# Taps of small levels for keys and values in common, wide additions of exps, and an unscaled token variance

## The chip, the cores and the metric

The kernel runs on one core of a Trainium2 chip. The metric is the device time of one execution in microseconds. Before the change the median of three runs was 3230.94 us (3228.27 to 3233.72). TensorE (PE) does matrix products, with weight loads (PEld) beside them; VectorE (DVE), ScalarE (ACT) and GpSimd (POOL) work on tiles; SyncE (SP) and GpSimd issue most of the DMA.

## The reference, cut to what matters

Eight images of 256 channels and 32 x 32 pixels go through two layers. Layer 0 is attention over a pyramid of keys and values, and it is where the change lies:

```python
q = einsum('bchw,oc->bohw', x, q_w)             # 8 heads of 32 channels
kv = einsum('bchw,oc->bohw', x, kv_w)           # key map, value map
def pooled(t):
    outs = []
    for i, r in enumerate([1, 2, 3, 6]):        # sides 32, 16, 11, 5
        p = average_pool(t, round(32 / r))
        p = p + depthwise_3x3(p, dconv_w[i], dconv_b[i])
        outs.append(p.reshape(B, C, -1))
    return concatenate(outs, axis=2)            # 1024 + 256 + 121 + 25 = 1426
k = layernorm(pooled(k_map).transpose(0, 2, 1), norm_w, norm_b)
v = layernorm(pooled(v_map).transpose(0, 2, 1), norm_w, norm_b)
att = softmax(q_g @ k.T * 32 ** -0.5) @ v       # per head, then a head mix, proj, residual
```

Here x is normalised by groups first. Layer 1 is single-head attention over the 1024 tokens of each image (width 256), then a network of eight experts that all run for every token, weighted by a gate. Everything is float32.

## The kernel before

The 256 channels lie on 128 partitions in two halves, c = 0 and 1. All queries, keys and values of layer 0 are made by batch b (one image). One batch is 45 steps: two halves c, two halves of the 1024 queries, and eleven key chunks of 128 (a unit is one c and one query half), plus one tail step for the last keys of all four units. In a step `scores` (line 1596) makes four heads' products into the single score buffer `sc` in PSUM, ScalarE takes their exp into a `pt` tile of 128 x 4 x 512 (six buffers), and `values` (1606) of the step before is accumulated in `pv`. So the next score has to wait for the exp to have read `sc`. Keys stand in tiles `kn`, value tokens in `vt`.

Beside the steps runs background work: preparing the next batch, and layer 1 of the last one (`layer1` at 1778, `outputs` at 1832). These are generators, called threads. The class `Flow` (662) is a planner: it keeps an estimated clock per engine and per tile, resumes the thread whose next operation is estimated to be ready, and so writes one fixed order for every engine. `step` (916) runs threads between scores within a credit of TensorE time; `finish` (929) runs them until something that is needed exists. Where it foresees a wait of over 1.8 us on TensorE, `warm` (844) writes filler, products of constants. Each engine then runs its order strictly one after another. Every recorded operation has line 675, so the profile tells them apart by tile names.

For a batch, `prepare` (1463) normalises x and pools it to sides 11 and 5; `maps` (1184) forms four maps by matmul (m = 2, 3 are values, 0, 1 keys) over pixels and the two small pooled levels; ScalarE copies each from PSUM into a map tile and writes the middle tap with bias into `acc`; `halve` (1163) makes the side-16 level on GpSimd. `convolve` (1357) calls `taps` (1327): eight operations of VectorE per level and map, each acc += tap * shifted map, for four levels, so each depends on the one before. The first batch has its own order (`first_maps`, `first_keys`, `first_taps`); TensorE does the large convolution of its keys.

`by_tokens` (1384) turns four key chunks of `acc` to tokens by transposes, takes their statistics on VectorE (`statistics`, 1369) and scales them on ScalarE. The reciprocal root is a power on GpSimd; `rstd` (1024) multiplies the summed variance by 1/C and adds eps on VectorE before it. `value_tokens` and `key_tokens` (1547, 1560) do so in three groups, of which g = 2 has the small levels.

For the softmax sums, an accumulating DMA from GpSimd's queue adds each odd chunk's exps to those of the even chunk before (`add`, 1651; `tail_add`, 1643), and `sums` (1658) adds the six resulting tiles on VectorE, each in two operations of 128 x 1024, before one product by ones. The first four units sum on TensorE instead.

After the last step the rest of layer 1 and the experts run. A branch at the end would repeat everything in a general form if the sums were out of bounds.

Of the kernel before, what the change touches and what calls it, by code (L numbers as in the profile page):

```python
# [25 lines left out]
NT = NK - (NKC - 1) * P  # L26
NE = 8
SCALE0 = DH ** -0.5
SCALE1 = C ** -0.5
FILLER = 5  # L30
# [15 lines left out]
KEY_CHUNKS = [(i * P, min(P, NK - i * P)) for i in range(NKC)]  # L46
# [102 lines left out]
def layer0_general(tc, kit, nb, x, t1, consts, consts8, vecs, q_t, kv_t, proj_t, gqk_t):  # L149
    nc = tc.nc  # L150
    T = kit.tile
    with ExitStack() as ctx:
# [189 lines left out]
        def transpose_values(b):  # L342
            acc = vs.pop(b)
            for i in range(0, NKC, 2):
                ps = T(psum, [P, 512], "sm")
                part = KEY_CHUNKS[i : i + 2]
# [14 lines left out]
        def global_token(b):  # L361
# [22 lines left out]
            for kc, (k0, w) in enumerate(KEY_CHUNKS):  # L384
                nc.tensor.transpose(ps[:w, kc * 8 : kc * 8 + 8], pg[:, k0 : k0 + w], ident[:HEADS, :HEADS])
            pt = T(work, [P, NKC * 8], "gpt")
            last, lw = (NKC - 1) * 8, KEY_CHUNKS[-1][1]
# [5 lines left out]
            for kc, (k0, w) in enumerate(KEY_CHUNKS):  # L393
                nc.tensor.matmul(
                    ps[:HEADS, :C],
                    lhsT=pt[:w, kc * 8 : kc * 8 + 8],
                    rhs=vext[:w, kc, :, 0::2, :],
                    start=kc == 0,
                    stop=kc == NKC - 1,
                )  # L400
# [144 lines left out]
        def attend(n, background, steps):  # L545
# [4 lines left out]
            for half in range(2):  # L550
# [14 lines left out]
                for kc, (k0, w) in enumerate(KEY_CHUNKS):  # L565
# [381 lines left out]
def attention(tc, kit, f, outer, ended, nb, consts, x, t1, t2, hn, bounds, vecs, q_t, kv_t, proj_t, gqk_t, wqk, wqkv, vecs1, w1_d, w1c, gate_d, wrc, vecs2, bnvec, w2_d, h2d, between, pre, held):  # L947
# [6 lines left out]
    with ExitStack() as ctx:  # L954
# [73 lines left out]
        def mix():  # L1028
# [79 lines left out]
            for c in range(2):  # L1108
                f.ve.tensor_scalar(mt[:, c, :], raw[:, c, :], vec[:, V_NW + c : V_NW + c + 1], None, ALU.mult)
# [20 lines left out]
        made = [0]  # L1130
# [32 lines left out]
        def halve(p, small_p, c, acc):  # L1163
# [7 lines left out]
            l2 = small_p.rearrange("p (h w) -> p h w", h=16)  # L1171
            f.pool.tensor_tensor(l2, t2[:, 0::2, :], t2[:, 1::2, :], ALU.add)
            pooling.clear()
            yield act(small_p)
            f.act.activation(
                acc[:, HW : OFFS[2]],
                small_p,
                AF.Identity,
                bias=db(c, 1),
                scale=mid[:, c * 4 + 1 : c * 4 + 2],  # L1180
            )
            halved.append(acc)

        def maps(xp):

            for m in (2, 3, 0, 1):
# [5 lines left out]
                acc = T(work, [P, NK], "acc", bufs=3)  # L1192
                for s0, w in MAP_SLICES:
                    if s0 >= HW:
                        yield until(lambda: len(done) >= len(todo) - 1)
                        f.spawn(halve(p, p[:, HW : OFFS[2]], c, acc), 1)
# [3 lines left out]
                    for k in range(2):  # L1200
# [6 lines left out]
                        )  # L1207
                    f.act.activation(p[:, s0 : s0 + w], ps[:, :w], AF.Copy)
                    for s, n in enumerate(SIDES):
                        a, z = max(OFFS[s], s0), min(OFFS[s] + n * n, s0 + w)  # L1210
                        if a < z:
                            f.act.activation(
                                acc[:, a:z],
                                ps[:, a - s0 : z - s0],
                                AF.Identity,
                                bias=db(c, s),
                                scale=mid[:, c * 4 + s : c * 4 + s + 1],
                            )
# [8 lines left out]
        pmaps = [T(pool_, [P, NK], f"map{i}") for i, pool_ in enumerate((between, work))]  # L1227
        for t in pmaps:
            f.split(t, 512, HW)
        first, large, whole, pooled, asked, halved = {}, [], [], [], [], []  # L1230
# [13 lines left out]
        def first_maps(xp):  # L1244


            for m in range(4):
                if m < 2:
                    p = T(work, [P, 4, 512], "pt", bufs=6).rearrange("p j q -> p (j q)")
                    acc = T(l1, [P, NK], "v") if m else T(work, [P, NK], "kn", bufs=3)  # L1250
                else:
                    p = pmaps[m - 2]
                    acc = T(work, [P, NK], "acc", bufs=3)
                for t in (p, acc):
                    if t is not p or m < 2:
                        f.split(t, 512, HW)
                first[m] = p, acc
            for m, s0 in [(m, s0) for m in (2, 3) for s0 in (0, 512)] + [
# [11 lines left out]
                for k in range(2):  # L1270
# [7 lines left out]
                small_levels = s0 > HW and m < 2  # L1278
                f.act.activation(
                    ptail[:, m, s0 - HW : s0 - HW + w] if small_levels else p[:, s0 : s0 + w], ps[:, :w], AF.Copy  # L1280
                )
                for s, n in enumerate(SIDES):
                    a, z = max(OFFS[s], s0), min(OFFS[s] + n * n, s0 + w)
                    if a < z and (m >= 2 or s):
                        f.act.activation(
                            acc[:, a:z],
                            ps[:, a - s0 : z - s0],
                            AF.Identity,
                            bias=db(c, s),
                            scale=mid[:, c * 4 + s : c * 4 + s + 1],  # L1290
                        )
                if s0 == 512:
                    f.spawn(halve(p, ptail[:, m, :256] if m < 2 else p[:, HW : OFFS[2]], c, acc), 0)
                if s0 == 512:
# [5 lines left out]
            whole.append("maps")  # L1300
# [26 lines left out]
        def taps(c, s, p, acc, base=0):  # L1327
            n, o = SIDES[s], OFFS[s]
            pin = p[:, o - base : o - base + n * n].rearrange("p (h w) -> p h w", h=n)
            pout = acc[:, o : o + n * n].rearrange("p (h w) -> p h w", h=n)  # L1330
            for tap in range(9):
                if tap == 4:
                    continue
                dy, dx, y0, y1, x0, x1 = windows(tap, n)
                o_ap = pout[:, y0:y1, x0:x1]
                yield ve(pin[:, y0 + dy : y1 + dy, x0 + dx : x1 + dx], o_ap)
                f.ve.scalar_tensor_tensor(
                    o_ap, pin[:, y0 + dy : y1 + dy, x0 + dx : x1 + dx], dw(c, s, tap), o_ap, ALU.mult, ALU.add
                )

        def first_taps():
# [5 lines left out]
            yield until(lambda: whole)  # L1347
            for m in (0, 1, 2, 3):
                p, acc = first[m]
                for s in range(1, 4):  # L1350
                    if s == 1:
                        yield until(lambda: acc in halved)
                    yield from taps(m % 2, s, *((ptail[:, m, :], acc, HW) if m < 2 else (p, acc)))
                whole.append(m)
            done.extend(first[m][1] for m in (2, 3, 0, 1))

        def convolve():

            for m in range(4, 4 * nb):
                yield until(lambda: len(todo) > m)  # L1360
                c, p, acc = todo[m]
                for s in range(4):
                    if s == 1:
                        yield until(lambda: acc in halved)
                    yield from taps(c, s, p, acc)
                    read[0] += s == 0
                done.append(acc)

        def statistics(st, n, eps, mean=None):
# [7 lines left out]
            f.ve.tensor_tensor(var, st[:, :, 2], st[:, :, 5], ALU.add)  # L1377
# [3 lines left out]
            rstd(r, var, eps, 1.0 / C)  # L1381
            return r

        def by_tokens(accs, dst, k0):

            chunks = KEY_CHUNKS[k0 : k0 + 4]
            st = T(work, [P, 4, 6], "tst", bufs=3)
            f.pool.memset(st, 1.0)
            for i in range(0, 4, 2):
                span = slice(chunks[i][0], sum(chunks[i + 1]))  # L1390
# [6 lines left out]
                w = chunks[i + 1][1]  # L1397
                if w == P:
                    f.act.activation(dst[:, i : i + 2, :], ps.rearrange("p (u c) -> p u c", u=2), AF.Copy)
                else:  # L1400
                    f.act.activation(dst[:, i, :], ps[:, :C], AF.Copy)
                    f.act.activation(dst[:w, i + 1, :], ps[:w, C:], AF.Copy)
# [60 lines left out]
        def prepare(b):  # L1463
# [42 lines left out]
            else:  # L1506
                yield from maps(xp)
# [1333 lines left out]
```

## Time and profile before

| | us |
|---|---|
| median of three runs | 3230.94 |
| profiled execution, its own time | 3231.56 |
| its span, first to last instruction | 3229.8 |
| start to first exp of layer 0 | 84.7 |
| first to last exp | 1755.8 |
| last exp to end | 1389.3 |
| TensorE busy in the span | 3071.1 |
| VectorE busy in the span | 2350.0 |
| ScalarE busy in the span | 1628.2 |

The profile is of one execution. A group is named by the tiles that it writes and reads, as `acc<-map,vec,acc` for a tap, `pt<-pt,pt` for an addition of exps, `sc<-q,kn` for scores, `sm<-con` for filler. A float32 product shows as two records. "Idle before" is time in which an engine had nothing running ahead of an operation, and the name behind the arrow is what ended that. Work on an engine that is not the bound costs time only if another engine waits for it.

### The profile page before, as it was taken

To read this page: it belongs to the slowest core of one execution; us is meant where nothing else is said; L and a number is where in the kernel's file an instruction comes from. 1 tells how busy PE (TensorE), PEld (TensorE's weight loads), DVE (VectorE), ACT (ScalarE), POOL (GpSimd) and SP (SyncE) were. 2 spreads that over 40 slices of the span, in tenths; PEclk is the share of its full clock that TensorE was granted. 3 is DMA by queue.
4 is the path that set the end of the run, shared out by engine and by line. 5 is a ranking of instruction groups with operands and counts; after the bars stand their busy time and mean duration, and the time that the engine had idled before them with its cause. 6 is when DMAs were issued, how large, how long until landed. Compare 5 with 4: busy or idle time off the path is not lost.

```text
span 3229.8 us, 57102 instructions
## 1 busy us (share of the span) xinstructions
PE 3071.1 (95%) x22958; PEld 1782.2 (55%) x22958; DVE 2350.0 (73%) x4196; ACT 1628.2 (50%) x2164; POOL 1183.1 (37%) x1273
## 2 busy tenths in 40 slices
PE   7889799989999999999999999999999999999998
PEld 4323233334333333433433367776888888888887
DVE  6973888878888788898544444445887888887776
ACT  3757666556666566656655423334333333334443
POOL 3323223132242232322121120003855556567766
PEclk9999999999999999999999999999999999999999
DMA  1367765565665575666776652224444345320000
GB/s 54 82 134 185 141 144 121 134 148 110 155 133 121 133 158 105 146 137 141 168 160 134 147 210 92 79 72 154 150 150 141 142 162 169 131 81 24 20 14 21
DMA packets 123346, 396.04 MB, mean 123 GB/s; under 512 B 15280, under 2 KB 41208, under 8 KB 99840
## 3 DMA queue, kind: packets, MB, share of 16 engines
q0 software_dynamic: 28608, 179.85, 28.7%
q1 hardware_dynamic: 90960, 210.46, 19.1%
q8 instruction: 183, 3.00, 0.4%
q10 hardware_dynamic: 3504, 1.99, 0.2%
q14 instruction: 91, 0.75, 0.1%
HBM read 129.77 MB, written 97.03 MB: 70 GB/s over the span
## 4 chain that ended last, share of the span: by engine, by line
PE 51%; DVE 5%; issue 2%; ACT 1%; POOL 1%; DMA 1%; DVEq 0%; ACTq 0%; POOLq 0%
PE bank L675 21%; PE sm L675 10%; PE y L675 10%; PE sx L675 3%; PE sc L675 3%; PE pv L675 3%; DVE h L675 2%; DMA pt<-pt 1%; ACT pt L675 1%; DVE u L675 1%; DVE pt L675 1%; DVE c L675 1%; POOL t L675 0%; DVE t L675 0%; DVE acc L675 0%
## 5 line engine op out<-in xcount | busy, mean ns | idle before, releaser
L675 ACT ACTIVATE pt<-sc 128x2048 f32<-128x2048 f32 x352 | 660.8, 1877 | 284.5 <-PE sc L675 226.8
L675 DVE SCALAR_TENSOR_TENSOR acc<-map,vec,acc 128x961 f32<-128x961 f32 (+3 forms) x960 | 561.2, 593 | 33.7 <-ACT acc L675 7.6
L675 DVE TENSOR_TENSOR pt<-pt,pt 128x1024 f32<-128x1024 f32 x280 | 350.7, 1298 | 193.6 <-DMA pt<-pt 177.9
L675 PE MATMUL sc<-q,kn 32*128 32x512 f32 (+1 forms) x3072 | 419.3, 647 | 68.6 <-ACT pt L675 62.2
L675 PE MATMUL pv<-pt,vt 128*32 128x512 f32 x2816 | 382.0, 615 | 2.2 <-ACT vt L675 2.2
L675 ACT ACTIVATE h<-h,bnvec 128x512 f32<-128x512 f32 x432 | 326.7, 805 | 64.9 <-DVE h L675 57.4
L675 POOL TENSOR_TENSOR rstd<-rstd,mhalf 128x4 f32<-128x4 f32 (+2 forms) x88 | 103.5, 1177 | 690.9 <-DVE rstd L675 625.6
L675 ACT ACTIVATE p1c<-bank 128x256 f32<-128x256 f32 x216 | 82.5, 382 | 541.9 <-PE bank L675 541.3
L675 POOL DMA_DIRECT2D pt<-pt x160 | 144.9, 909 | 441.2 <-ACT pt L675 331.6
L675 DVE TENSOR_TENSOR h<-p1c,bank 128x512 f32<-128x512 f32 x216 | 147.2, 681 | 197.4 <-PE bank L675 191.9
L675 PEld LDWEIGHTS sc<-q,kn 32*128 32x128 f32 (+1 forms) x3072 | 113.6, 178 | 246.6 <-ACT pt L675 137.0
L675 DVE TENSOR_TENSOR h<-u,bank 128x256 f32<-128x256 f32 (+1 forms) x432 | 219.8, 550 | 7.4
L675 POOL TENSOR_TENSOR tm<-h,tm 128x256 f32<-128x256 f32 x190 | 217.6, 1145 | 14.9
L675 PEld LDWEIGHTS pv<-pt,vt 128*32 128x32 f32 x2816 | 56.0, 109 | 275.2 <-issue 259.5
L675 DVE TENSOR_TENSOR h<-h,gate 128x1024 f32<-128x1024 f32 x128 | 194.4, 1519 | 0.9 <-ACT h L675 0.5
L675 POOL TENSOR_TENSOR tm<-h 128x512 f32<-128x512 f32 x95 | 121.5, 1279 | 186.0 <-ACT h L675 186.0
L675 PE MATMUL y<-t,s3e 128*128 128x256 f32 x768 | 187.0, 380 | 2.0 <-POOL t L675 2.0
L675 PE MATMUL sm<-y,t 128*32 128x256 f32 (+1 forms) x1992 | 182.9, 387 | 3.7 <-DVE res L675 2.5
L675 PE MATMUL bank<-t,s1e 128*128 128x256 f32 x726 | 176.6, 379 | 0.0
L675 POOL TENSOR_TENSOR t<-h 128x512 f32<-128x512 f32 x98 | 124.5, 1270 | 132.4 <-DVE h L675 100.1
L675 DVE TENSOR_TENSOR u<-h,bank 128x512 f32<-128x512 f32 x216 | 148.5, 687 | 23.3 <-PE bank L675 0.5
L675 PE MATMUL bank<-h,w2e 128*128 128x256 f32 (+1 forms) x480 | 161.5, 466 | 2.4 <-DVE h L675 2.4
(374 smaller groups left out, 5513.8 us busy)
## 6 DMA issues: line engine op xcount, KB each, us to landing
pt<-pt POOLq DMA_DIRECT2D x160, 1024.0 KB, 7.8
h<-h SPq DMA_DIRECT2D x175, 512.0 KB
xi<-in_x_dram SPq DMA_DIRECT2D x16, 512.0 KB
t<-t SPq DMA_DIRECT2D x8, 1024.0 KB
res<-t SPq DMA_DIRECT2D x32, 256.0 KB
t<-res SPq DMA_DIRECT2D x32, 256.0 KB
hn<-res SPq DMA_DIRECT2D x32, 256.0 KB
hn<-hn SPq DMA_DIRECT2D x16, 512.0 KB
```

The lines of the kernel that those rows point to most:

```text
L675: ins = fn(*args, **kwargs)
```

## The change

It has three parts.

1. The three small levels of keys and values of one channel half lie together. A tile `small{c}` of 836 columns has, for each level of side n, the value map of n rows, one row of zeros, and the key map of n rows: 2n+1 rows (33 x 16, 23 x 11, 11 x 5). Its accumulator is `sacc{c}`. One tap then covers both maps. GpSimd sets the zero rows (`small_maps`), `join` writes the middle tap with bias once all four contributions are there, and `small_taps` runs after the four large levels of the batch. Large maps and their `acc` shrink to 1024 columns. The last two key chunks become 121 and 25 keys instead of 128 and 18, so that they are the levels of side 11 and 5. Value tokens g = 2 wait until the units of the batch before have passed chunk 3; `vt` has five buffers in place of six, `tst` two in place of three.
2. `sums` adds a pair of exps over all 2048 columns in one operation (121 rows for the last).
3. For tokens, the summed variance is not divided by C; eps * C is added in an operation that was there, and the power is taken of it at once. Normalised tokens are then smaller by sqrt(C) = 16: the exps' scale for keys and the weights `mt` behind the values hold the factor `SPREAD`.

```diff
-NT = NK - (NKC - 1) * P
+NT = 25
+NS = (0, 528, 781, 836)
+SPREAD = C ** 0.5
-KEY_CHUNKS = [(i * P, min(P, NK - i * P)) for i in range(NKC)]
+ALL_CHUNKS = [(i * P, min(P, NK - i * P)) for i in range(NKC)]
+KEY_CHUNKS = [*ALL_CHUNKS[:-2], (OFFS[2], OFFS[3] - OFFS[2]), (OFFS[3], NT)]
...
+        def small_maps(b, c):
+            yield until(lambda: len(convolved) >= 2 * b - 2 + c + 1)
+            t = smaps[b, c] = T(work, [P, NS[3]], f"small{c}")
+            for s in range(1, 4):
+                f.pool.memset(level(t, s)[:, SIDES[s] : SIDES[s] + 1, :], 0.0)
+            counts[b, c] = 0
+            f.spawn(join(b, c), 1)
+        def join(b, c):
+            yield until(lambda: counts[b, c] == 4 and (b == 0 or {(b - 1, 0), (b - 1, 1)}.issubset(marks)))
+            yield act(smaps[b, c])
+            acc = T(work, [P, NS[3]], f"sacc{c}")
+            for s in range(1, 4):
+                a, z = NS[s - 1], NS[s]
+                f.act.activation(acc[:, a:z], smaps[b, c][:, a:z], AF.Identity, ...)
+            joined[b, c] = acc
+        def copy_small(ps, b, c, keys):
+            for s in (2, 3):
+                ...
+                f.act.activation(level(smaps[b, c], s, keys), src.rearrange("p (h w) -> p h w", w=n), AF.Copy)
+            counts[b, c] += 1
...
-        def taps(c, s, p, acc, base=0):
+        def taps(c, s, p, acc):
+            rows = 2 * n + 1 if s else n
...
+        def small_taps(b):
+            for c in range(2):
+                yield until(lambda: (b, c) in joined)
+                for s in range(1, 4):
+                    yield from taps(c, s, smaps[b, c], joined[b, c])
+                convolved.append((b, c))
...
-            for m in range(4, 4 * nb):
-                yield until(lambda: len(todo) > m)
-                c, p, acc = todo[m]
-                for s in range(4):
-                    if s == 1:
-                        yield until(lambda: acc in halved)
-                    yield from taps(c, s, p, acc)
-                    read[0] += s == 0
-                done.append(acc)
+            for b in range(1, nb):
+                for m in range(4 * b, 4 * b + 4):
+                    yield until(lambda: len(todo) > m)
+                    c, p, acc = todo[m]
+                    yield from taps(c, 0, p, acc)
+                    read[0] += 1
+                    done.append(acc)
+                yield from small_taps(b)
...
-            f.ve.tensor_tensor(var, st[:, :, 2], st[:, :, 5], ALU.add)
+            if mean is None:
+                f.ve.tensor_tensor(var, st[:, :, 2], st[:, :, 5], ALU.add)
+            else:
+                f.ve.scalar_tensor_tensor(var, st[:, :, 2], eps * C, st[:, :, 5], ALU.add, ALU.add)
...
-            rstd(r, var, eps, 1.0 / C)
+            if mean is None:
+                rstd(r, var, eps, 1.0 / C)
+            else:
+                f.pool.tensor_tensor(r, var, kit.mhalf[:, 0:1].to_broadcast([P, n]), ALU.pow)
...
+            if g == 2:
+                yield until(lambda: len(convolved) >= 2 * b + 2 and (b == 0 or spent[0] >= 4 * b))
+                accs = [joined[b, c] for c in range(2)]
...
-            f.act.activation(pt[:w], t[:w], AF.Exp, scale=SCALE0)
+            f.act.activation(pt[:w], t[:w], AF.Exp, scale=SCALE0 * SPREAD)
...
-                for j in range(0, 4, 2):
-                    s = pairs[0][:, j : j + 2, :]
-                    yield ve(s, pairs[i])
-                    f.ve.tensor_tensor(s, s, pairs[i][:, j : j + 2, :], ALU.add)
+                s = pairs[0][: rows[i]]
+                yield ve(s, pairs[i])
+                f.ve.tensor_tensor(s, s, pairs[i][: rows[i]], ALU.add)
```

## The prediction

> **What bounds the kernel now.** I read the page first (engines, slices), then the stretches by stage, then the waits of TensorE, then single stretches of the timeline.
>
> The page's first two parts: busy time of each engine, and its tenths in 40 slices.
>
> ```profile
> PE 3071.1 (95%) x22958; PEld 1782.2 (55%) x22958; DVE 2350.0 (73%) x4196; ACT 1628.2 (50%) x2164; POOL 1183.1 (37%) x1273
> ...
> PE   7889799989999999999999999999999999999998
> ...
> DVE  6973888878888788898544444445887888887776
> ```
>
> TensorE is near full everywhere; the change touches layer 0, the first 23 slices, where VectorE shows 7 to 9. By stage (start to first exp, first to last exp, rest), columns span, busy PE, PEld, DVE, ACT, POOL, then clock and DMA:
>
> ```profile
> 0.00:84.70 84.70, 66.49 (x204) 35.10 (x204) 55.28 (x120) 34.28 (x71) 32.14 (x42) 0.96 0.16 52
> 84.70:1840.50 1755.80, 1644.61 (x16769) 629.70 (x16772) 1326.83 (x2601) 1100.04 (x1282) 466.16 (x529) 0.98 0.64 138
> 1840.50:3229.80 1389.30, 1359.96 (x5992) 1117.35 (x5984) 967.92 (x1477) 493.84 (x812) 684.83 (x703) 1.00 0.31 107
> ```
>
> In the attention stage TensorE is busy 1644.6 of 1755.8 us, so all that fewer waits can give there is 111.2 us. VectorE has 1326.8 us (75.6%) and isn't the bound on its own. TensorE's waits, total, times, longest:
>
> ```profile
> PE sc L675 <- ACT pt L675: 62.2, 65, 4.9
> ...
> PE sx L675 <- DMA pt<-pt: 7.6, 5, 3.3
> PE sm L675 <- DVE acc L675: 5.1, 1, 5.1
> ```
>
> The 111.2 us split by length: 42.7 us in 71 gaps of about 1.0 us before scores (nothing else was ready, so TensorE waits for the exp); 25.1 us in 10 longer gaps before scores; 36.4 us in 18 longer gaps before background matmuls; 7 us of crumbs. What a long one looks like, in order of time:
>
> ```profile
> 1100.00 0.17 DVE L675 TENSOR_SCALAR rstd<-var 128x4 f32<-128x4 f32 x1
> ...
> 1102.29 1.05 PE L675 MATMUL sm<-con 128*32 128x256 f32 x16
> ...
> 1102.79 2.36 DVE L675 TENSOR_TENSOR pt<-pt,pt 128x1024 f32<-128x1024 f32 x2 [1.96 <-DMA pt<-pt]
> 1105.07 0.16 DVE L675 SCALAR_TENSOR_TENSOR tshift<-tmean,rstd 128x4 f32<-128x4 f32 x1
> ...
> 1105.32 1.09 ACT L675 ACTIVATE kt<-kt,tshift,rstd 128x256 f32<-128x256 f32 x2 [4.38 <-DVE tshift L675]
> 1106.32 1.85 ACT L675 ACTIVATE pt<-sc 128x2048 f32<-128x2048 f32 x1
> ...
> 1108.22 1.24 PE L675 MATMUL sc<-q,kn 32*128 32x512 f32 x4 [4.89 <-ACT pt L675]
> ```
>
> A 0.16 us VectorE operation (tshift) stands behind two pair additions; ScalarE's kt stands behind it, the exp behind kt, and TensorE idles 4.89 us. The 1.05 us of `sm<-con` before it is filler: products of constants which the planner writes where it foresees a wait. So VectorE costs time as a queue, not by its sum.
>
> [...] the 1024 additions have a median of 1218 ns, and the taps below have a fixed part of about 0.24 us. I go by the trace's rows for taps[...].
>
> **The change part by part.** Rows for the taps (busy us, mean ns):
>
> ```profile
> L675 DVE SCALAR_TENSOR_TENSOR acc<-map,vec,acc 128x992 f32<-128x992 f32 x120 | 154.5, 1288 | 3.4
> L675 DVE SCALAR_TENSOR_TENSOR acc<-map,vec,acc 128x240 f32<-128x240 f32 x120 | 58.3, 486 | 3.7
> L675 DVE SCALAR_TENSOR_TENSOR acc<-map,vec,acc 128x225 f32<-128x225 f32 x120 | 55.8, 465 | 2.9
> L675 DVE SCALAR_TENSOR_TENSOR acc<-map,vec,acc 128x110 f32<-128x110 f32 x120 | 43.9, 366 | 3.9
> L675 DVE SCALAR_TENSOR_TENSOR acc<-map,vec,acc 128x20 f32<-128x20 f32 x120 | 31.7, 264 | 4.0
> ```
>
> 1. Small levels in common. Before: 32 maps x 24 taps = 768 operations, per map 4 x (486 + 465 + 366 + 358 + 264 + 253) ns = 8.77 us (358 and 253 from the rows of 100 and 16 elements), 280.6 us in all. After: 16 half-channels x 24 = 384, over 2n+1 rows. On the straight line between neighbouring rows 512, 495 and 480 elements cost 776, 758, 742 ns; 242, 230, 220 cost 488, 477, 468; 50, 44, 40 cost 298, 291, 287. With 2, 2 and 4 taps of each: 6.04 + 3.80 + 2.33 = 12.16 us, x16 = 194.6. Saved: 86 us of VectorE.
>
> 2. A pair of exps in one addition: 140 operations of 2048 in place of 280 of 1024. The two halves run back to back in 2.36 us (above)[...]. Gain[...] taken 0.1 x 140 = 14. It holds VectorE in one piece for 2.3 us, as two neighbours did before, so nothing late is made later. The first four units, summed on TensorE, are unchanged.
>
> 3. Tokens' variance: 48 operations `rstd<-var` of 170 ns go (8.1 us, partly overlapped; taken 6). GpSimd's power now reads the single variance buffer, so the next tokens' VectorE operation can wait for it. The built order shows one explicit new wait, before the first step, where TensorE has 15 us of key convolution ahead of it: nothing.
>
> Sum on VectorE: 86 + 14 + 6 = 106 us, 1326.8 to 1221.
>
> 4. ScalarE: per map the 121 and 25 scaled copies (460, 386 ns), the 146 copy (290) and the 256 one (601) go, 1.74 us x32 = 56. In place come two plain copies per map, of 121 and 25 (estimate 0.27 and 0.19 from the slope of the copies of 256 and 512, 382 and 596 ns), 15 us; three joins per half-channel (0.83, 0.60, 0.42), 30 us; one more key copy of 25 in 16 places, 3 us. That is 8 us less of 1100, hidden either way.
>
> 5. GpSimd: 48 memsets more, 0.1 to 0.36 us (the row of 24 elements), about 10 us of 466. In the built order they stand 20 or more steps behind the taps that free their buffer, so GpSimd, and the accumulating DMAs queued behind them, don't wait. The tail's DMA adds 25 rows for 18 (4.2 us to landing, small), vz takes 25 rows for 18: nothing.
>
> 6. What moves. Small levels now follow all large ones, and their value tokens wait for the last unit of the batch before. In the built order the small taps of a batch end at step 14 to 22 of the 45 of the batch before, the keys' last group by step 33, the values' by step 42; they are needed from step 8 of their own batch. At 4.9 us a step that is 50 us of cover; without it, each batch would lose the tail of such a chain, about 5 us. In the old order one batch had its last keys at its own step 2.
>
> 7. TensorE. Scores, values, projections and layer 1 are the same work. Fillers fall from 81 to 24 matmuls: the 81 took 12.3 us in the trace, 24 narrow ones take 3.1 (8 in 1.05 us above, two records each). That is 9 us less, wherever the planner was right that a wait has gone. About 11 us of layer-1 matmuls move from the last stage into the attention stage, without changing the sum.
>
> Idle time. Pricing each step's matmuls by the trace's rows, steps with no background work rise from 31 to 39, steps with under 0.9 us fall from 59 to 53; filling all up to 3.2 us would take 38 us before, 40 after: +2. The long waits, 61.5 us, come of queues on VectorE; I scale them as load/(1 - load), 0.756 giving 3.1 and 0.70 giving 2.4: 23% less, 14 us. That rule is a choice; its ends are no gain and two thirds gone (41 us).
>
> Sum: -9 - 14 + 2 = -21 us against the profiled execution's 3231.6 (span 3229.8), 3210.6; the median shown is 3230.9, so 3210.
>
> **Rivals.** (a) VectorE's load isn't what makes the waits long, they are mistakes of the planner that come again in any order: for it, the DMA and ScalarE links in the chain above; against it, the tshift queue. Then -9 + 2: 3224. (b) Slower: the new order packs the background. Steps with over 8 us of matmuls rise from 21 to 30, most right after a batch begins, and steps with none from 31 to 39. If the 71 short gaps grow in that ratio (42.7 x 8/31 = 11 us), packed steps delay additions and so the exps' buffers by 2 us at each of seven batch starts (14), and nothing but the 9 us of fillers is won: +16, 3247. It decides from 0.6 us a batch start on, where 11 + 7 x 0.6 - 9 passes 6 us. The 4.06 us gap at 1209.84, five us into the sixth batch, where an exp stood behind a pair addition, speaks for it; the earlier tokens speak against. (c) Two thirds of the long waits go: -48, 3183. That the wide addition runs as two would cost 3 us of idle at most; that is inside each case.
>
> **Numbers.** Chances: 0.48 for 3210 (3197 to 3221), 0.20 for (a), 0.20 for (b), 0.12 for (c). The range 3184 to 3246 leaves the outer half of (b) and (c). 0.2% (6.5 us) is what a measurement of this kernel tells from no change: case (a) lies on that border and is halved, so faster 0.68, same 0.12, slower 0.20.
>
> **What would show it.** In the changed profile: VectorE near 1220 us between first and last exp; tap rows of 512 near 0.78 us and of 40 near 0.29; an addition of 2048 near 2.3 us; filler under 4 us; TensorE's idle there near 99 us, with long gaps near 47. Small levels' tokens should hold up no score. I'm wrong if long gaps stay at 60 us with VectorE relieved, if they gather at batch starts, or if taps over 2n+1 rows cost more than the line between their neighbours.

## The result

| | median us | lowest to highest | executions |
|---|---|---|---|
| before | 3230.94 | 3223.00 to 3236.76 | 17 |
| after | 3239.63 | 3232.20 to 3248.27 | 17 |

The ratio is 1.0029, 95% interval 1.0020 to 1.0039: the change made the kernel slower by 8.7 us where 21 us less was forecast. The profiled execution of after took 3234.14 us (span 3231.5), one of its quicker ones; its rows tell what the work became, and the 8.7 us are settled by the medians.

The page of after, busy time of the engines:

```profile
PE 3058.1 (95%) x22550; PEld 1779.9 (55%) x22550; DVE 2255.1 (70%) x3624; ACT 1622.9 (50%) x2164; POOL 1212.5 (38%) x1321
```

VectorE has 95 us less than before (2350.0). So the work did go. TensorE is busy for 13.0 us less than before (3071.1), 9.2 of them filler, and in this execution idles 14.7 us more (173.4 for 158.7). Its stretches by stage, columns as for before:

```profile
0.00:86.65 86.65, 67.11 (x196) 34.88 (x196) 55.28 (x106) 33.54 (x69) 33.19 (x49) 0.94 0.16 51
86.65:1855.56 1768.91, 1641.52 (x16444) 637.70 (x16447) 1235.69 (x2063) 1095.71 (x1286) 487.74 (x573) 0.98 0.64 138
1855.56:3231.50 1375.94, 1349.49 (x5916) 1107.28 (x5911) 964.14 (x1457) 493.62 (x810) 691.55 (x700) 1.00 0.31 108
```

Between first and last exp VectorE fell from 1326.8 to 1235.7 us, yet the stage grew by 13.1 us, to 1768.9. TensorE is busy in it for 1641.5, so it is idle for 127.4 us, where it was 111.2. The last stage is 13.4 us shorter: 10.5 us of TensorE's work of layer 1 moved ahead. Split as for before, the 127.4 us are 45.8 in 78 short gaps before scores (42.7 in 71 before), 28.8 in 14 long ones, over 1.1 us, before scores (25.1 in 10), 42.6 in 17 long ones before background work (36.4 in 18), and 10.2 of crumbs. The long ones grew most, and they don't gather at batch starts. The longest is 8.5 us, half as much as the whole growth of 16 us; the longest before was 4.9. It lies 117 us into the stage, a gap in which TensorE's own sum of an early unit waits for accumulating DMAs of exps. The two that were issued from 186 to 214 us, beside transfers of x, q and weights, took 14.0 us to land, where the median of the run is 8.0. The profile of small levels alone, a run below, has the same gap (8.5 us).

Waits of TensorE in the whole span, and the largest wait of VectorE (total, times, longest):

```profile
PE sc L678 <- ACT pt L678: 70.7, 72, 4.7
PE sm L678 <- DVE res L678: 13.6, 9, 4.0
PE sx L678 <- DMA pt<-pt: 10.5, 2, 8.5
```

```profile
DVE pt L678 <- DMA pt<-pt: 271.5, 73, 15.6
```

VectorE now stands for 271.5 us at a pair addition whose accumulating DMA hasn't landed; before, the same row was

```profile
DVE pt L675 <- DMA pt<-pt: 177.9, 70, 9.8
```

It has more time, and spends it at the head of its queue. What that does to others, in order of time:

```profile
876.40 1.07 PE L678 MATMUL pv<-pt,vt 128*32 128x512 f32 x8
...
877.56 2.29 DVE L678 TENSOR_TENSOR pt<-pt,pt 128x2048 f32<-128x2048 f32 x1 [1.27 <-DMA pt<-pt]
879.76 0.69 DVE L678 TENSOR_TENSOR sm<-sm,rec 128x512 f32<-128x512 f32 x1
880.49 0.88 DVE L678 SCALAR_TENSOR_TENSOR res<-sm,bv,res 128x256 f32<-128x256 f32 x2
...
881.42 1.11 PE L678 MATMUL sm<-con,acc 128*128 128x128 f32 x4 [3.96 <-DVE res L678]
```

An addition waits 1.27 us for its DMA, runs for 2.29, and the two operations behind it, which free the PSUM bank, come late: TensorE idles 3.96 us. It is the picture that the prediction showed of before, with other names. So what had to be settled is why an emptier VectorE queue still made such gaps.

### The profile page after: what moved, and what is told of

It is laid out like the page before. It is cut to its first block, busy times and chain, and to the rows that moved or that the text cites. A ratio compares the mean times of both kernels' runs of the same rounds, so it can differ in the third digit from the quotient of the medians.

```text
span 3231.5 us, 55789 instructions
## 1 busy us (share of the span) xinstructions
PE 3058.1 (95%) x22550; PEld 1779.9 (55%) x22550; DVE 2255.1 (70%) x3624; ACT 1622.9 (50%) x2164; POOL 1212.5 (38%) x1321
## 5 line engine op out<-in xcount | busy, mean ns | idle before, releaser
L678 ACT ACTIVATE pt<-sc 128x2048 f32<-128x2048 f32 (+1 forms) x352 | 660.3, 1876 | 333.4 <-PE sc L678 276.1
L678 DVE TENSOR_TENSOR pt<-pt,pt 128x2048 f32<-128x2048 f32 (+1 forms) x140 | 322.8, 2306 | 290.4 <-DMA pt<-pt 271.5
L678 PE MATMUL sc<-q,kn 32*128 32x512 f32 (+2 forms) x3072 | 419.2, 650 | 74.8 <-ACT pt L678 70.7
L678 PE MATMUL pv<-pt,vt 128*32 128x512 f32 (+1 forms) x2816 | 382.4, 615 | 0.1
L678 DVE SCALAR_TENSOR_TENSOR acc<-map,vec,acc 128x961 f32<-128x961 f32 (+1 forms) x240 | 315.6, 1317 | 43.0 <-ACT acc L678 37.3
L678 PEld LDWEIGHTS sc<-q,kn 32*128 32x128 f32 (+2 forms) x3072 | 113.0, 178 | 256.5 <-ACT pt L678 152.6
L678 DVE SCALAR_TENSOR_TENSOR sacc<-small,vec,sacc 128x480 f32<-128x480 f32 (+8 forms) x384 | 205.7, 543 | 14.6 <-ACT sacc L678 4.4
L678 POOL TENSOR_TENSOR rstd<-rstd,mhalf 128x2 f32<-128x2 f32 (+1 forms) x40 | 52.3, 1307 | 430.3 <-DVE rstd L678 360.3
L678 PEld LDWEIGHTS pv<-pt,vt 128*32 128x32 f32 (+1 forms) x2816 | 55.8, 108 | 273.3 <-issue 260.6
L678 PE MATMUL sm<-p,v 128*32 128x256 f32 (+1 forms) x2320 | 194.0, 383 | 1.9 <-DVE rec L678 1.9
```

Source lines behind the costliest of these rows:

```text
L678: ins = fn(*args, **kwargs)
```

## The experiments

The kernel before took 3229.8 to 3231.2 us (medians) on the chips of all these runs; each ratio is to that. "Order" is the sequence of instructions that the planner wrote on each engine.

### Is VectorE's work worth anything, if nothing else moves?

The order of the kernel before is held on every engine; small-level taps cover only two rows of each map (the rest of their convolution is left out), while the planner still counts them whole.

```diff
+                if s:
+                    f.planned = (y1 - y0) * (x1 - x0)
+                    y1 = y0 + 2
+                    o_ap = pout[:, y0:y1, x0:x1]
                 f.ve.scalar_tensor_tensor(o_ap, pin[...], dw(c, s, tap), o_ap, ALU.mult, ALU.add)
+                f.planned = None          # cost() takes it in place of the size
```

> The kernel before, with its order on every engine kept instruction for instruction; each tap of a small level covers only two rows of its level, so VectorE has some 75 us less to do (the rest of these levels is left without that tap). Theory Q (VectorE's load makes the long waits of TensorE): 14 us or more faster, 3217 us or less, and the long gaps of TensorE in the attention stage fall from 61 us to under 48. Theory O (the written order and the planner's errors make them, not the load): within 4 us of before, long gaps still near 60 us.

Measured: 3210.53 us, ratio 0.9942 (0.9929 to 0.9955). Its attention stage:

```profile
84.32:1818.81 1734.49, 1633.08 (x16769) 626.65 (x16772) 1255.40 (x2601) 1100.76 (x1282) 465.03 (x529) 0.99 0.65 140
```

VectorE has 71.4 us less than before, the stage 21.3 less: 9.8 of idle time (111.2 to 101.4) and 11.5 of TensorE's busy time for the same 16769 records. The last goes with the granted clock, 0.99 in this stage where the kernel before had 0.98: by the estimate at the end, its cost fell from 29.0 to 17.4 us. Long gaps fell from 61.5 to 54.2 us, not under the 48 that theory Q had. So VectorE's load does cost time in an order that stays, and more than the prediction gave it (14 us for 106); half of it is busy time that goes with the clock (11.6 us by that estimate), which the prediction left out.

### The three parts, each alone

Wide additions alone:

```diff
-                for j in range(0, 4, 2):
-                    s = pairs[0][:, j : j + 2, :]
-                    yield ve(s, pairs[i])
-                    f.ve.tensor_tensor(s, s, pairs[i][:, j : j + 2, :], ALU.add)
+                s = pairs[0]
+                yield ve(s, pairs[i])
+                f.ve.tensor_tensor(s, s, pairs[i], ALU.add)
```

> The kernel before with the wide additions of exps alone; the planner writes a new order. Theory Q: VectorE some 10 us less, 1 to 4 us faster. Theory O: the new order is as good as chance makes it, 3223 to 3250 us, with no relation to VectorE's load. If this part carries the loss of the whole change (one long operation in front of short ones): 3238 or more.

Measured: 3252.43 us, ratio 1.0071 (1.0058 to 1.0084): just above the range of theory O.

The unscaled variance alone (the diffs of `statistics`, `SPREAD` and the exps' scale on the kernel before):

```diff
-            f.ve.tensor_tensor(var, st[:, :, 2], st[:, :, 5], ALU.add)
+            f.ve.scalar_tensor_tensor(var, st[:, :, 2], eps * C, st[:, :, 5], ALU.add, ALU.add)   # tokens
-            rstd(r, var, eps, 1.0 / C)
+            f.pool.tensor_tensor(r, var, kit.mhalf[:, 0:1].to_broadcast([P, n]), ALU.pow)         # tokens
```

> The kernel before with the unscaled variance of tokens alone; the planner writes a new order. Theory Q: one operation of 0.17 us less on the way to the tokens, 0 to 3 us faster. Theory O: 3223 to 3250 us, as chance makes it, although next to nothing is taken away.

Measured: 3237.30 us, ratio 1.0023 (1.0013 to 1.0033).

Small levels in common alone, which is the changed kernel with the two other parts taken back (the diffs above, reversed):

```diff
-                s = pairs[0][: rows[i]]
-                yield ve(s, pairs[i])
-                f.ve.tensor_tensor(s, s, pairs[i][: rows[i]], ALU.add)
+                for j in range(0, 4, 2):
+                    s = pairs[0][: rows[i], j : j + 2, :]
+                    yield ve(s, pairs[i])
+                    f.ve.tensor_tensor(s, s, pairs[i][: rows[i], j : j + 2, :], ALU.add)
```

> The changed kernel with additions in halves and the scaled variance again, so the small levels' part alone. Theory Q: 86 us of VectorE less, 10 us faster than before or more. If this part carries the loss by packing the background (rival b): 3238 or more, with the idle time at the starts of batches. Theory O: 3223 to 3250 us, gaps spread over the stage.

Measured: 3218.44 us, ratio 0.9961 (0.9950 to 0.9973): faster than both kernels, as theory Q said. So the loss lies in what comes with the additions and the variance, the two parts to which the prediction gave 20 us less VectorE and no cost.

### The long operation, or the order?

The wide operation in the old order: the planner is told of two halves, as before, and the instruction is issued once, at the second.

```diff
                 for j in range(0, 4, 2):
                     s = pairs[0][:, j : j + 2, :]
                     yield ve(s, pairs[i])
-                    f.ve.tensor_tensor(s, s, pairs[i][:, j : j + 2, :], ALU.add)
+                    if j:
+                        f.planned = 1024
+                        f.ve.tensor_tensor(pairs[0], pairs[0], pairs[i], ALU.add)
+                        f.planned = None
+                    else:
+                        f.note("DVE", "tensor_tensor", None, (s, s, ...), {})   # counted, not issued
```

> The kernel before with its order on every engine kept; where the two halves of a pair addition stood next to each other, one addition of 2048 stands. Theory H (the long operation itself holds up short ones): most of the 22 us that wide additions alone cost is here, 3245 or more. Theory O (the new order that the planner wrote costs them): 3224 to 3232, the operation itself giving some 0.07 us each.

Measured: 3231.54 us, ratio 1.0003 (0.9994 to 1.0011).

And two halves in the order that wide additions alone had given:

```diff
-                f.ve.tensor_tensor(s, s, pairs[i], ALU.add)
+                f.note("DVE", "tensor_tensor", None, (s, s, pairs[i]), {})
+                for j in range(0, 4, 2):
+                    h = pairs[0][:, j : j + 2, :]
+                    f.chained("DVE", f.ve.eng.tensor_tensor(h, h, pairs[i][:, j : j + 2, :], ALU.add))  # issued, not counted
```

> The order that the planner wrote for wide additions alone, with two halves in the place of each. Theory H: back to some 3231. Theory O: still 3248 or more.

Measured: 3250.66 us, ratio 1.0058 (1.0044 to 1.0072). The two stages side by side, first the wide operation in the old order, then wide additions alone:

```profile
84.27:1835.99 1751.72, 1638.67 (x16769) 628.13 (x16772) 1315.18 (x2463) 1100.40 (x1281) 486.53 (x529) 0.99 0.64 138
```

```profile
83.62:1860.64 1777.02, 1653.77 (x16661) 635.35 (x16664) 1305.76 (x2478) 1100.58 (x1281) 479.94 (x532) 0.98 0.63 137
```

The same additions; VectorE is busy 9 us less in the second, and its stage is 25.3 us longer: 10.2 of idle TensorE, 15.1 of busy TensorE for fewer records. So the operation costs nothing that can be told (-2 to +4 us by the interval of its run), and the order costs some 20. What makes the order differ is one number: `cost` gives two halves 2 x (0.15 + 0.00107 x 1024) = 2.49 us, and one wide operation 0.15 + 0.00107 x 2048 = 2.34. With one wide operation estimated at 2.49 us, the planner writes the old order, operation by operation; with two halves estimated at 1.17 each, it writes the new one, but for one exchange on ScalarE.

### Filler

All 81 filler products are left out, and the order of the kernel before is held.

```diff
-            self.pe.matmul(t[:, :C], lhsT=self.kit.ones, rhs=self.kit.con[:, :C], start=True, stop=True)
+            o, l, r = t[:, :C], self.kit.ones, self.kit.con[:, :C]
+            for j in range(0, P, DH) if self.narrow(l, r) else [None]:
+                a = (o, l) if j is None else (o[j : j + DH], l[:, j : j + DH])
+                self.note("PE", "matmul", None, a, {"rhs": r})   # counted, not issued
```

> The kernel before with its order kept and all 81 filler products left out. By the prediction's seventh step (12 us of filler are work that TensorE is spared): up to 12 us faster. Theory C (filler stands where TensorE waits anyway[...]): no faster, 0 to 10 us slower, and the mean granted clock falls below the 0.988 of before.

Measured: 3227.64 us, ratio 0.9993 (0.9986 to 1.0000). The filler took 12.3 us in the profile of before, and leaving it out gave some 2 us (0 to 4.5 by the interval), so much of it stands in waits. The mean granted clock is 0.987 (21 executions), where the kernel before has 0.988.

### The changed kernel with its additions in halves

The changed kernel, with the edit shown for small levels alone on the additions only.

> The changed kernel with the additions in halves again, the planner writing a new order. Theory H: the wide additions' cost is gone, 3215 to 3222. Theory O: no relation to the single parts, anything from 3215 to 3245.

Measured: 3232.74 us, ratio 1.0009 (0.9998 to 1.0019): 6.9 us less than the changed kernel, 14.3 more than small levels alone. Theory H, 3215 to 3222, missed. A wide operation estimated at 2.49 us gives this same order in the changed kernel too.

### How far apart do orders lie for the same work?

One estimate of the planner is moved by 0.01 us. Nothing else changes but filler.

```diff
         if op == "scalar_tensor_tensor":
-            return 0.23 + 0.00103 * n
+            return 0.24 + 0.00103 * n      # "taps"
...
-        return 0.15 + 0.00107 * n
+        return 0.16 + 0.00107 * n          # "others": additions of exps among them
```

The kernel before, taps and then others:

> The kernel before; the only edit is the planner's own estimate of a tap: 0.24 us + 0.00103 per element in place of 0.23. No instruction is added or removed but for filler; the planner writes another order. Theory O (the planner's order is a draw: orders for the same work lie some 20 us apart, and the order of the kernel before is a good one): another time, more than 5 us from 3231, likelier slower, 3237 to 3260. Theory T (the order answers only to what the change does, not to a hundredth of a microsecond in an estimate): 3231 within 3 us.

> The kernel before; the only edit is the planner's estimate for VectorE's other operations with a second operand or out of PSUM: 0.16 us + 0.00107 per element in place of 0.15. The same two theories: O, more than 5 us from 3231, likelier slower, 3237 to 3260; T, 3231 within 3 us.

Measured: 3221.35 us, ratio 0.9976 (0.9969 to 0.9982), and 3234.63 us, 1.0020 (1.0011 to 1.0028). The first moved by more than 5 us, as theory O said, but to the faster side; the second lies between the two theories.

The changed kernel, taps and then others:

> The changed kernel with the estimate of a tap at 0.24 us in place of 0.23, nothing else. Theory O: another time, more than 5 us from 3239, anywhere from 3215 to 3255; and if 91 us less of VectorE's work are worth the 20 us of the pinned order, such draws lie lower than those of the kernel before do. Theory T: 3239 within 3 us.

> The changed kernel with the estimate of VectorE's other operations at 0.16 us + in place of 0.15 (which moves its additions of 2048 by nothing beside their 2.3 us). If only draws decide: 3215 to 3245, and with the two others a mean near 3225. If the wide additions cost 20 us whatever the draw: 3230 to 3245.

Measured: 3223.14 us, ratio 0.9976 (0.9969 to 0.9983), and 3229.82 us, 0.9995 (0.9987 to 1.0003). The same instructions but for filler take 16.5 and 9.8 us less than in the changed kernel; in the profiles of these two, TensorE's idle time in the attention stage is 108.2 and 109.2 us, where the changed kernel has 127.4.

Small levels alone, taps and then others:

> Small levels in common alone (which took 3218.4), with the estimate of a tap at 0.24 us in place of 0.23, nothing else. Theory O: 3218 was a good draw, now 3220 to 3245. Theory T (small levels alone are a gain of 12 us, and the additions and the variance give it back): 3218 within 3 us.

> Small levels in common alone, with the estimate of VectorE's other operations at 0.16 us + in place of 0.15. The kernel before took 3234.6 under this nudge. If small levels are worth some 20 us on the mean of the orders (the pinned order's value; the two pairs so far gave 12 and 24): 3203 to 3225. If the two low times were lucky draws: anywhere from 3215 to 3250, mean 3235.

Measured: 3197.03 us, ratio 0.9899 (0.9884 to 0.9914), and 3217.94 us, 0.9962 (0.9948 to 0.9976). The first is the fastest kernel of this study, and faster than either theory had it; the second is where small levels worth 20 us would put it. The attention stage of the first:

```profile
85.30:1817.05 1731.75, 1639.25 (x16657) 638.72 (x16660) 1255.22 (x2248) 1095.57 (x1286) 480.32 (x572) 0.99 0.65 142
```

TensorE's idle time is 92.5 us, 18.7 less than before.

Wide additions alone, taps:

> Wide additions alone (3252.4 without a nudge), with the planner's estimate of a tap at 0.24 us in place of 0.23. If the loss of 22 us was one draw of the order: another time, by up to 20 us nearer to the 3221 that the kernel before gave under this nudge, below 3240. If a planner that has to place operations of 2.3 us whole always writes poorer orders: about 22 us over 3221, 3240 to 3255.

Measured: 3253.89 us, ratio 1.0073 (1.0059 to 1.0087). The loss of the wide additions' order was no single draw: under the same nudge the kernel before has 3221.35.

### Work put back into the changed order

The changed kernel's order is held on every engine, and each of the 128 taps of side 16 is followed by one of the same shape that adds zero times its input.

```diff
                 f.ve.scalar_tensor_tensor(o_ap, i_ap, dw(c, s, tap), o_ap, ALU.mult, ALU.add)
+                if s == 1:
+                    f.chained("DVE", f.ve.eng.scalar_tensor_tensor(o_ap, i_ap, p[:, n * n : n * n + 1], o_ap, ALU.mult, ALU.add))
```

> The changed kernel with the order that the planner wrote for it held on every engine, and VectorE's work put back: each of the 128 taps of side 16 is followed by one of the same shape that adds zero times its input, 97 us by the rows of the profile, against the 91 us that the change took away. The planner does not count them. If less work of VectorE is worth 20 us in this order as it was in the order of before, the time rises by 15 to 35 us, to 3255 to 3275: then the changed order with the old load would be far poorer than the old order. If this order does not use the relief: under 3245.

Measured: 3304.28 us, ratio 1.0223 (1.0209 to 1.0237).

```profile
89.81:1929.89 1840.08, 1669.83 (x16448) 644.52 (x16450) 1325.81 (x2184) 1095.35 (x1285) 491.74 (x574) 0.96 0.61 133
```

The rise of 65 us is nearly twice what even the dearer case had said, and this row tells most. VectorE is busy for 1325.8 us in the stage, the same as in the kernel before (1326.8), and the stage is 84 us longer. So the changed order does use the relief: with as much work as before, put back in this place, it is far slower than the old order.

With 90 us more than the planner counted, the stage grew by 71; with 71 us less than counted (short taps in the old order) it shrank by only 21. That this holds wherever the work stands isn't shown. The work went back in one place, behind the taps of side 16, while it had come from many. All of the 42.9 us by which TensorE's idle time grew lie in the stretches of small taps (breaks under 3 us joined) and the 8 us behind each (43.5 us in the changed kernel, 91.6 here). Its second longest wait in the stage,

```profile
PE sx L678 <- DVE pt L678: 12.4, 2, 8.7
```

8.7 us, ends 33 us of VectorE (from 1553.6 to 1586.3) in which a single pair addition stood between the taps.

### The changed kernel with the old estimate

The changed kernel with taps at 0.24 us, as above, and its wide additions estimated at the 2.49 us of two halves:

```diff
+                f.planned = 2187
                 f.ve.tensor_tensor(s, s, pairs[i][: rows[i]], ALU.add)
+                f.planned = None
```

> The changed kernel with the estimate of a tap at 0.24 us (3223.1 so far), and with its additions of 2048 planned at the 2.49 us that two halves were planned at, in place of 2.34. No instruction differs otherwise but for filler. If the estimate of 2.34 us made the planner's orders poorer in each case so far: 3196 to 3216, near the 3197 of small levels alone under this nudge. If it is only draws: 3215 to 3240.

Measured: 3200.01 us, ratio 0.9910 (0.9897 to 0.9924). All three parts of the change are in it, and it is 23.1 us faster than with the estimate of 2.34. Its attention stage:

```profile
84.88:1840.81 1755.93, 1653.82 (x16565) 645.36 (x16568) 1238.45 (x2086) 1098.68 (x1289) 497.81 (x578) 0.98 0.65 140
```

VectorE has the changed kernel's load there (1238.5 us, 1235.7 in the profile of after) and TensorE the same work and more, and it idles 102.1 us instead of 127.4. Beside the same nudge with the estimate of 2.34, TensorE idles 17.4 us less over the whole span (142.4 for 159.8) and is busy for 9.8 less. So the order alone can win or lose what the change was to bring.

Small levels alone with taps estimated at 0.28 us, nearer to the durations measured for large taps:

```diff
-            return 0.23 + 0.00103 * n
+            return 0.28 + 0.00103 * n
```

> Small levels in common alone, with the estimate of a tap at 0.28 us + 0.00103 per element: 1.302 us for 992 elements, of which the profile measured 1.288 before and 1.333 after. With 0.23 it took 3218.4, with 0.24 3197.0. If estimates that run ahead of the chip are what makes orders poor: no more than 3200. If 3197 was a good draw: 3203 to 3230.

Measured: 3215.18 us, ratio 0.9960 (0.9946 to 0.9975). So an estimate nearer to the chip isn't what made 3197; the expectation's other reading, a good draw, stands.

### All draws together

Medians in us, by the estimates that the planner used:

| | unchanged | taps 0.24 | others 0.16 | taps 0.28 |
|---|---|---|---|---|
| before | 3230.9 | 3221.4 | 3234.6 | |
| wide additions alone | 3252.4 | 3253.9 | | |
| small levels alone | 3218.4 | 3197.0 | 3217.9 | 3215.2 |
| small levels and variance, or all three with additions at 2.49 | 3232.7 | 3200.0 | | |
| the change, additions at 2.34 | 3239.6 | 3223.1 | 3229.8 | |

(The first entry of the fourth row is the run with halves, the second that with the wide operation.) Down the columns: small levels gain 12.5, 24.4 and 16.7 us, mean 18. The shorter estimate of the additions loses 22 and 33 us without small levels, 7 and 23 with them, in four of four. The variance loses 6 alone, 14 with small levels, 3 with them under taps at 0.24 (there with the wide operation). The whole change is +9, +2 and -5: on the mean nothing.

## Why the prediction was wrong

- **What bounds it; step 1.** Right in kind. VectorE as a queue does cost TensorE time: 71 us less of it in a held order gave 20 us. VectorE's saving in the stage was 91 us where 106 were forecast. Small levels' part of it was mis-sized: the new tap rows, means and sums of one profile,

```profile
L678 DVE SCALAR_TENSOR_TENSOR sacc<-small,vec,sacc 128x480 f32<-128x480 f32 x64 | 47.1, 735 | 5.9 <-ACT sacc L678 4.4
...
L678 DVE SCALAR_TENSOR_TENSOR sacc<-small,vec,sacc 128x220 f32<-128x220 f32 x64 | 32.8, 513 | 1.3
L678 DVE SCALAR_TENSOR_TENSOR sacc<-small,vec,sacc 128x512 f32<-128x512 f32 x32 | 25.5, 797 | 0.9
...
L678 DVE SCALAR_TENSOR_TENSOR sacc<-small,vec,sacc 128x40 f32<-128x40 f32 x64 | 22.9, 358 | 1.6
```

  with the other five come to 208.5 us where 194.6 were forecast, a saving of 72 and not 86. The line between neighbours was right for most of the operations (the median of the 40-element taps is 260 ns, for 287 forecast); their mean is raised by a few long ones, six of 64 over 0.8 us. (For 220 and 230 elements the line was drawn past the row of 225, which makes 0.6 us.) The large taps, which the change leaves alone, took 315.6 us where they had taken 306.0.
- **Step 2.** The operation was sized well:

```profile
L678 DVE TENSOR_TENSOR pt<-pt,pt 128x2048 f32<-128x2048 f32 x112 | 258.7, 2310 | 275.9 <-DMA pt<-pt 271.5 <-ACT pt L678 4.0 <-issue 0.3
```

  2310 ns on the mean (median 2292), where the prediction looked for some 2.3 us. The 0.1 us a pair that the step took as its gain was the author's estimate. Held in the old order the operation takes 11.6 us off VectorE in the stage (1326.8 to 1315.2) and costs nothing that can be told, as the step says. But "so nothing late is made later" was said of the instruction in an order that is given, and the kernel's order isn't given: the planner's estimate fell by 0.15 us per addition, it wrote another order on every engine, and that one cost 7 us here and up to 33 in the other pairs. The prediction consulted the built order for what was moved on purpose, and put the rest of it at nothing.
- **Step 3** (6 us less VectorE). Taken alone it cost 6 us, and 14 and 3 beside small levels. The new wait that the step names isn't the reason, for it comes once (the row is of the changed kernel):

```profile
DVE var L678 <- POOL rstd L678: 0.9, 1, 0.9
```

  Its order is the likely one, but no run has the variance in the old order, so the runs don't tell an effect of its own from a draw.
- **Step 4** holds: ScalarE 1095.7 us for 1092 forecast. **Step 5** was too low: GpSimd rose by 21.5 us, not 10, to 487.7. The wide operation in the old order, which adds no memset, already had 486.5. **Step 6** holds: TensorE waits once for a small level's accumulator (`sacc`), 0.6 us.
- **Step 7, fillers.** Their sum did fall from 12.3 to 3.1 us. Counting that as 9 us gained was wrong: leaving all of them out of the old order gave 2 us.
- **Idle time, the step that failed** (-14 by load/(1 - load), +2 for bare steps). Idle time in the stage rose by 16 us to 127.4, and didn't fall to 99; long gaps went from 61.5 to 71.4, not 47. The rule scaled the gaps of the old order, so it took the new order to be as good for the new load as the old one was for the old, and put the order itself at nothing. The profiles, one of each kernel, show what stood in its place: 107.8 us of idle time in the stage with small levels alone, 116.8 with the variance added, 127.4 with the wide additions too, where VectorE's load fell from 1248.4 to 1238.4 and 1235.7. The medians rise with it: 3218.4, 3232.7, 3239.6. With the order held the rule does well: for the short taps (a load of 0.724) it gives 9 us, and idle time fell by 9.8. But the 111.2 us weren't all that fewer waits can give, since TensorE's busy time fell by 11.5 more with the clock, and the 71 short gaps were 0.6 us long on the mean, not 1.0.
- **Rivals.** (a) gave the nearest account: the planner's mistakes come again in any order. But its 3224 counted 9 us for filler, and its other half, that VectorE's load doesn't matter, fell with the first experiment. (b) had the right sign by a wrong mechanism: gaps don't gather at batch starts, and short gaps rose by 3 us, not 11. (c), -48, was reached by no run; the best draw of small levels alone gave 33 us.
- **The measured 8.7 us** are within the range but have the sign that had a fifth of the chance. (Halving (a) makes 0.70 for faster and 0.10 for the same, not 0.68 and 0.12.) What was missing was a term for the order itself. The draws of one and the same kernel span 13 us (before), 17 (after) and 21 (small levels alone), which is as much as the forecast gain.

What stays open: why the shorter estimate of the additions gave a poorer order in four of four. It isn't that the planner was too hopeful, for 2.34 us is nearer to the measured 2.31 than 2.49 is, and a tap estimate nearer to the chip didn't help either. Four draws out of orders that spread by 20 us can still be chance. Nor does any run separate the fewer buffers (`vt` and `tst`) from the rest of small levels' part.

## What to carry to other kernels

Where a program writes the order, a change of one operation is two changes: the operation, and every order that follows from its estimated cost. Hold the order to price the operation, then move an estimate by a hundredth of a microsecond a few times to see how far orders spread for the same work; a gain below that spread can't be forecast from one build, but the best of several builds can be kept (here 3197 and 3200 us against 3231). Time freed on an engine that isn't the bound is spent by the planner before the chip sees it: the order that it writes for the lighter load need not carry the old load as well as the old order did.

## What the runs showed of the hardware

Where TensorE waited, the granted clock often added to the cost; in two of the four pairs of runs below what it cost changed by more than the idle time did (11.6 us for 9.8, 12.7 for 10.2). In the attention stage the clock was at 0.5 within 3.41 us of the end of 11 of the 15 waits of over 2 us in the profile of before, and of 9 of the 13 in that of after. In the changed kernel, eight records of the same shape, before the largest gap and behind it:

```profile
191.50 1.04 PE L678 MATMUL sx<-pt,con 128*32 128x512 f32 x8
...
211.96 1.94 PE L678 MATMUL sx<-pt,con 128*32 128x512 f32 x8 [8.50 <-DMA pt<-pt]
```

They took 1.04 us at a clock of 1.00, and 1.94 at 0.50, where it stood from 208.6 to 215.4 us.

In the profiles of before and after, each stretch at 0.5 but the last lasts 3.41, 6.83 or 10.24 us, and the stretches begin at whole multiples of 3.41 us from one another. Behind a wait of 1.93 us, at 974.5 us of the profile of before, the clock was 0.50 from 977.8 to 984.6. Behind one of 3.04 us, at 1671.3 of after, it stayed at 1.00. So the length of the wait doesn't decide alone, and no run shows what else does.

What this cost is estimated as half of the time for which TensorE was busy at a clock of 0.5, since the eight records above took nearly twice as long there; in the kernel before, 57.9 us of the stage give 29.0. By the traces, in the attention stage:

| | idle time, us | busy time, us | cost of the clock, us |
|---|---|---|---|
| short taps in the old order, for before | -9.8 | -11.5 | 17.4 for 29.0 |
| order of wide additions, for the old order | +10.2 | +15.1 | 34.8 for 22.1 |
| work put back, for the changed kernel | +42.9 | +28.3 | 51.8 for 25.1 |
| the change, for before | +16.2 | -3.1 | 25.1 for 29.0 |

In the first three rows the work of TensorE is nearly the same on both sides, and the clock's cost makes most of what its busy time changed by (11.6 of 11.5 us, 12.7 of 15.1, 26.7 of 28.3). But there is no fixed price: in the last row idle time grew by 16.2 us, and the clock cost 3.9 less. Over all executions the mean clock is 0.9883 for the kernel before (48 executions) and 0.9855 for the changed one (17). That goes the way of the 8.7 us but doesn't account for them: the variance alone has 0.9891 and is slower than before, the kernel before with taps at 0.24 has 0.9873 and is faster, and no run changed the clock by itself.
